# Score rows of single-head layers through VectorE and DRAM instead of TensorE, and a second, transposed load of adj

## Chip, cores, metric

The kernel runs on one core of a Trainium2 chip. The metric is device time in microseconds for one launch over all 128 graphs; the number compared is the median of repeated runs.

## What is computed

There are 128 graphs of 128 nodes with 512 features, x[128, 128, 512], and an integer adjacency matrix adj[128, 128, 128]. Each graph goes through four attention layers, every one of the form x = x + layer(relu(layernorm(x))). All is float32.

```
h = relu(layernorm(x))
layer 0:  s[i,j] = leaky(f1[i] + f2[j]), f = h W^T a;  masked where adj == 0;  softmax over j;  x += elu(att @ h)
layer 1:  4 heads of 256: s[i,j] = leaky(src[i] + dst[j]); mask adj > 0 or i == j; softmax over the SOURCE i
          (so the mask is needed transposed);  y = elu(att^T @ (h W1) + b1)
          then one head of 512 on y, same mask;  x += that + b2
layer 2:  one head: leaky(h.w_src[i] + h.w_dst[j] + b); mask adj + eye != 0; softmax over j;  x += att @ h
layer 3:  8 heads of 64: leaky(a_src[i] + a_dst[j] + b); mask adj > 0; softmax over j;  x += relu(att @ (h Wp))
```

## The kernel before

**Staging.** Weights stay in SBUF. One graph at a time is a *stream*: the generator `graph(b)` (line 920) yields single instructions (`Step`), groups of them, and takes of buffers. Up to FLYING = 11 graphs are in flight, and a twelfth is loaded ahead. All x tiles are 128 nodes (partitions) by 512 features.

**What sets the order.** No instruction is placed by hand. A greedy planner, `Scheduler` (line 140), keeps for every engine the time at which it comes free and for every tile the time at which it is written, both from cost formulas in `Step.estimate` (line 61). `issue()` (line 241) takes, out of the next steps of all streams, the one that can start first; a tie goes to the stream with the earlier due time (`rank`), and due times come from a rehearsal of one graph. What it emits is a fixed order for each engine; at run time each engine waits in that order. The transfers of SP (plain DMAs) and POOL (accumulating DMAs) are part of it: SP too executes its DMA issues in order and waits before each for its data. In the planner all transfers share one pipe (`moved`).

**Score rows.** A score needs f2[j] along the free axis, in all 128 partitions. There are two ways in the kernel:
- *TensorE*: a transpose of the column broadcast to 128 columns gives the row in a PSUM bank. `attended` (line 667) does so for layers 0, 2 and the second part of layer 1, and `add_rows` (line 587) for eight or sixteen columns at the end.
- *DRAM*: `rows_in_dram` (line 567) transposes 32x32 squares on VectorE, writes them to DRAM with four small DMAs, and a DMA broadcasts the result to 128 partitions. The four heads of layer 1 and the heads of layer 3 use this, except in the last LATE = 5 graphs.

`attention` (line 614) then adds row and mask and takes the maximum on VectorE (one operation with an accumulator for each head: a tensor_tensor_reduce, which the profile lists as CUSTOM_DVE_ANT_0 and DVE_READ_ACCUMULATOR2_ANT), and ScalarE does leaky relu and exp.

**Layer 3** (line 822) holds two times eight heads of 128x128 in one tile `sd`: `d` (rows by mask, for the maximum) and `e` (transposed). ScalarE copies the masks into both halves, one POOL DMA of 1024 KB adds all sixteen rows onto them with accumulation, VectorE reduces `d` to the maximum mx, and a second POOL DMA adds -mx onto `e`.

**Masks.** adj is loaded for four graphs at once (`load`, line 904). m0, m3 and m2 come from it on VectorE; the transposed masks m1 and m3t come from one TensorE transpose of m3 (lines 929 to 937). m3t lives from layer 1 to layer 3, in 11 buffers.

**Norm.** `norm_relu` (line 502): statistics on VectorE, reciprocal root on POOL, then nmr = -mean x rstd on VectorE, relu with scale and bias on ScalarE.

**Turn.** After layer 1's softmax `turned` (line 547) transposes the squares on VectorE and exchanges them through DRAM (four writes `turned<-e`, one read `et<-turned`).

**Buffers** that the text names: h (4), x2 (2; the projected y of layer 1's second part, held until its attention is done), e0 (3), r (5), sd (3).

Of the kernel before, what the change touches and what calls it, by code (L numbers as in the profile page):

```python
# [21 lines left out]
FLYING = 11  # L22
AHEAD = 1
# [19 lines left out]
class Step:  # L43
# [4 lines left out]
    def __init__(self, engine, method, args, kw):  # L48
        self.engine = engine
        self.calls = [(method, args, kw)]  # L50
        named = dict(kw)
        outs = [named.pop("out")] if "out" in named else [args[0]]
        if "accum_out" in named:
            outs.append(named.pop("accum_out"))
        ins = list(args[1:] if "out" not in kw else args) + list(named.values())
        ins = [a for a in ins if isinstance(a, bass.AP)]
        self.writes = [a.tensor.name for a in outs]
        self.reads = [a.tensor.name for a in ins]
        self.busy, self.delay = self.estimate(method.__name__, outs, ins, kw)

    def estimate(self, name, outs, ins, kw):

        if name == "dma_start":
            moved = size(outs[0]) * outs[0].shape[0] * 4
            if self.engine == "POOL":
                self.moves = moved / 165e3
                return 1.0, 3
            run = 4 * min(a.shape[-1] for a in outs + ins)
            self.moves = moved / (280e3 if run > 512 else 220e3)
            return (0.5 if max(len(a.shape) for a in outs + ins) > 2 else 0.35), 1.5  # L70
# [68 lines left out]

class Scheduler:  # L140
    def __init__(self):
        self.streams = []
        self.engine_free = {}
        self.written = {}
        self.moved = 0.0
        self.returned = {}
        self.tag_of = {}
        self.last_use = {}
        self.reached = set()
        self.pace = 0.0  # L150
        self.due = None
# [80 lines left out]
    def start(self, step):  # L232
        t = self.engine_free.get(step.engine, 0.0)
        for r in step.reads:
            t = max(t, self.written.get(r, 0.0))
        for w in step.writes:
            if w not in self.last_use:
                t = max(t, self.written.get(w, 0.0))
        return t

    def issue(self):
# [5 lines left out]
        if not ready:  # L247
            assert not self.streams, [vars(s.next) for s in self.streams]
            return False
        t, _, _, _, s = min(  # L250
            (self.start(s.next), self.rank(s), s.age, i, s) for i, s in enumerate(ready)
        )
        step = s.next
# [4 lines left out]
        end = t + step.busy + step.delay  # L258
        if step.moves:

            self.moved = max(end, self.moved) + step.moves
            end = self.moved + 0.3
        for name in step.writes:
            self.written[name] = end
        for name in step.reads + step.writes:
            self.last_use[name] = max(end, self.last_use.get(name, 0.0))
# [17 lines left out]
def kernel(  # L284
# [40 lines left out]
    small = ctx.enter_context(tc.tile_pool(name="small", bufs=FLYING + 2))  # L325
# [17 lines left out]
    def column(tag, n=1):  # L343
        return small.tile([P, n], F32, tag=tag, name=tag)

# [5 lines left out]
    off_diag = const.tile([P, P], F32, name="off_diag")  # L351
    nc.vector.tensor_scalar(off_diag, ident, -1.0, 1.0, ALU.mult, ALU.add)
# [36 lines left out]
    def setup():  # L389
# [6 lines left out]
        w0 = yield tile_of("sd", 3, 2 * H3, P)  # L396
        w0 = w0.rearrange("p s q -> p (s q)").rearrange("p (c f) -> p c f", c=KC)
        for c in range(KC):
            yield S.dma_start(out=w0[:, c], in_=l0_w[c * P : (c + 1) * P])
# [4 lines left out]
        yield Fork(fold_w1())  # L404
        yield from load(1)
# [19 lines left out]
        wa = yield tile_of("sd", 3, 2 * H3, P)  # L425
        wa = wa.rearrange("p s q -> p (s q)")[:, : H3 * 2 * K3]
# [5 lines left out]
    def fold_u(w0):  # L432
        us = [(yield bank()), (yield bank())]
        for c in range(KC):
            for i, u in enumerate(us):
                yield T.matmul(
                    u,
                    lhsT=a0[:, c, i : i + 1].to_broadcast([P, P]),
                    rhs=w0[:, c, :],
                    start=(c == 0),  # L440
                    stop=(c == KC - 1),
                )
# [3 lines left out]
        give_back(w0)  # L446
# [39 lines left out]
    def fold_w3(wa):  # L486
        pairs = wa.rearrange("p (h k) -> p h k", h=H3)
        for w in wpx:
            for s in range(2):
                prod = yield tile_of("t3", 2, D)  # L490
# [11 lines left out]
    def norm_relu(xt):  # L502
# [9 lines left out]
        yield V.scalar_tensor_tensor(nmr, mean, -1.0, rstd, ALU.mult, ALU.mult)  # L512
# [69 lines left out]

    def repeated(cols):
        n = cols.shape[1]
        return cols.unsqueeze(1).to_broadcast([P, Q // n, n])

    def add_rows(cols, to):

        for g in range(0, cols.shape[1], 4):
            pt = yield bank()  # L590
            yield Group(
                [
                    T.transpose(
                        pt[:, j * P : (j + 1) * P],
                        cols[:, g + j : g + j + 1].to_broadcast([P, P]),
                        ident,
                    )
                    for j in range(4)
                ]
            )  # L600
# [4 lines left out]
    def added(cols, to, late, rows=None):  # L605

        if late:
            yield from add_rows(cols, to)
            return
        if rows is None:  # L610
            rows = yield from rows_in_dram(repeated(cols), cols.shape[1])
        yield G.dma_start(out=to, in_=rows, accum_op=ALU.add)

    def attention(own, rows, e, mask, exact=False):
# [4 lines left out]
        mx = column(f"mx{nh}", nh)  # L619
# [18 lines left out]
        neg = column(f"neg{nh}", nh)  # L638
        yield V.scalar_tensor_tensor(neg, mx, -1.0, own, ALU.mult, ALU.subtract)
        nm = column(f"nm{nh}", nh)  # L640
        yield V.scalar_tensor_tensor(nm, neg, SLOPE, neg, ALU.mult, ALU.min)
        z = column(f"z{nh}", nh)
# [20 lines left out]
        rz = column(f"rz{nh}", nh)  # L663
        yield V.reciprocal(rz, z)
        return rz

    def attended(own, other, mask, values, exact=False):

        e = yield tile_of("e0", 3, P)
        pb = yield bank()  # L670
        yield T.transpose(pb[:, :P], other.to_broadcast([P, P]), ident)
        rz = yield from attention(own, [pb[:, :P]], [e], mask, exact)
# [5 lines left out]
        return pa, rz  # L678
# [39 lines left out]
    def layer0(xt, mask):  # L718
        h = yield from norm_relu(xt)
        yield Until("u")  # L720
        f = column("f0", 2)
        yield from dot(h, u1, f[:, 0:1])
        yield from dot(h, u2, f[:, 1:2])
        t = yield tile_of("t0", 2, D)
        pa, rz = yield from attended(f[:, 0:1], f[:, 1:2], mask, h, exact=True)
        give_back(h)

        yield A.activation(out=t, in_=pa, func=AF.Exp, scale=rz)
        yield A.activation(out=pa, in_=pa, func=AF.Relu, scale=rz)
        yield V.scalar_tensor_tensor(t, t, 1.0, pa, ALU.min, ALU.add)  # L730
# [4 lines left out]
    def layer1(xt, mask, late):  # L735
# [22 lines left out]
        rz = yield from attention(fx[:, H1:E1], heads, heads, mask)  # L758
        for j in range(H1):
            yield A.activation(out=heads[j], in_=heads[j], func=AF.Copy, scale=rz[:, j : j + 1])  # L760
        if late:
# [7 lines left out]
        for g in range(0, FC, 4):  # L769
# [23 lines left out]
            t = yield tile_of("t1", 2, 4 * P)  # L793
# [11 lines left out]
        pa, rz = yield from attended(gx[:, 1:2], gx[:, 0:1], mask, gx[:, E2:])  # L805
        give_back(gx)
        yield V.scalar_tensor_tensor(xt, pa, rz, xt, ALU.mult, ALU.add)
        give_back(pa)

    def layer2(xt, mask):  # L810
        h = yield from norm_relu(xt)
        f = column("f0", 2)
        yield from dot(h, w_src, f[:, 0:1])
        yield from dot(h, w_dst, f[:, 1:2])
        fb = column("fb")
        yield G.tensor_tensor(fb, f[:, 0:1], b_l2, ALU.add)
        pa, rz = yield from attended(fb, f[:, 1:2], mask, h)
        give_back(h)
        yield V.scalar_tensor_tensor(xt, pa, rz, xt, ALU.mult, ALU.add)
        give_back(pa)  # L820

    def layer3(xt, mask, mask_t, late):
# [10 lines left out]
        sd = yield tile_of("sd", 3, 2 * H3, P)  # L833
        d, e = sd[:, :H3], sd[:, H3:]
        for to, m in (d, mask), (e, mask_t):
            yield A.copy(to, m.unsqueeze(1).to_broadcast([P, H3, P]))
            give_back(m)
# [9 lines left out]
        f = small.tile([P, 2, H3], F32, tag="f3", name="f3")  # L847
        yield G.tensor_tensor(f, fx[:, :, :E3].rearrange("p h s -> p s h"), b_l3, ALU.add)
        fork = yield Fork(
            added(f.rearrange("p s h -> p (s h)"), sd.rearrange("p s q -> p (s q)"), late)  # L850
        )
        yield Join(fork)

        mx = column("mx3", H3)
        yield V.tensor_reduce(mx, d, AX.X, ALU.max)
        yield V.tensor_tensor(mx, mx, f[:, 1], ALU.add)
        yield A.activation(out=mx, in_=mx, func=AF.Prelu, alpha=SLOPE)
        yield V.tensor_scalar(mx, mx, -1.0, None, ALU.mult)
# [9 lines left out]
        rows = (yield Join(fork)) if fork else None  # L868
        fork = yield Fork(added(mx, e.rearrange("p h q -> p (h q)"), late, rows))
        yield Join(fork)  # L870
        ef = e.rearrange("p h q -> p (h q)")
        yield A.activation(out=ef, in_=ef, func=AF.Exp)
        t = yield tile_of("t3", 2, D)
        rz = column("rz3", H3)
# [24 lines left out]
        give_back(sd, fx)  # L899
# [4 lines left out]
    def load(b):  # L904
# [3 lines left out]
        if b % AG == 0:  # L908
# [3 lines left out]
            )  # L912
        sched.reached.add(("x", b))

    def not_above_0(a):
        m3 = yield tile_of("m3", 4, P)
        yield V.tensor_scalar(m3, a, 0.0, NEG, ALU.is_le, ALU.mult)
        return m3

    def graph(b):  # L920
        if FLYING + AHEAD <= b + AHEAD < B:
            yield Fork(load(b + AHEAD))
        yield Until(("x", b))
# [3 lines left out]
        yield from layer0(xt, m0)  # L927
        give_back(m0)
        m3 = yield from not_above_0(a)
        m3t = yield tile_of("m3t", FLYING, P)  # L930
        m1 = yield tile_of("m1", 8, P)
        pt = yield bank()
        yield T.transpose(pt[:, :P], m3, ident)
        give_back(m3)
        yield V.tensor_tensor(m1, pt[:, :P], off_diag, ALU.mult)
        yield A.copy(m3t, pt[:, :P])
        give_back(pt)
        yield from layer1(xt, m1, b >= B - LATE)
# [4 lines left out]
        yield from layer2(xt, m2)  # L943
        give_back(m2)
        m3 = yield from not_above_0(a)
        yield from layer3(xt, m3, m3t, b >= B - LATE)
        yield S.dma_start(out=out[b], in_=xt)

    adjs, xs = {}, {}
    with tc.manual_schedule():  # L950
        sched.rehearse(load(0))
        sched.plan(sched.rehearse(graph(0)))
# [59 lines left out]
```

## Time and profile before

| | |
|---|---|
| median of 3 runs | 3317.16 us (3317.16 to 3318.29) |
| profiled execution | 3315.37 us, of which the span of the profile is 3313.6 |
| TensorE (PE) busy | 3278.1 us, 99%; granted clock 0.992 |
| VectorE (DVE) busy | 2657.6 us, 80% |
| ScalarE (ACT) busy | 2600.8 us, 78% |
| GpSimd (POOL) busy | 954.6 us, 29% |
| DMA | 380.75 MB, 115 GB/s |
| transposes on TensorE by what they read | h 1024, e 404, f 336, x 128, m 128, mx 40 |

Busy time is the union of an engine's instructions, which overlap at their ends, so durations of a group add up to more than the engine's busy time. What an instruction occupies is read from the distance to the next start in the order of time. All lines of the page that name L256 come from the one call in the planner's `issue()`; groups are told apart by the tiles' names.

### The profile page before, as it was taken

The page shows a single profiled execution, that of the slowest core. Times are in us where ns is not written, and L with a number is a line of the kernel's source. Part 1 is how long each engine was busy: PE and PEld are TensorE (multiplying, and loading weights), DVE is VectorE, ACT ScalarE, POOL GpSimd, SP SyncE. Part 2 cuts the span into 40 slices and gives each one's busy share as a digit, 9 for nine tenths or more (in the row PEclk, how much of TensorE's full clock was granted, in tenths as well). Part 3 has the DMA queues.
Part 4 walks back from the last instruction along what each step waited for, and adds up shares of the span by engine and source line. Part 5 has one row for each costly group of instructions (what it writes and reads, how often), then busy time and mean ns, then how long its engine had stood idle before and what let it go on. Part 6 is the DMA issues. An engine that isn't in the chain of part 4 may idle for free.

```text
span 3313.6 us, 57764 instructions
## 1 busy us (share of the span) xinstructions
PE 3278.1 (99%) x16252; PEld 2577.0 (78%) x16252; DVE 2657.6 (80%) x9921; ACT 2600.8 (78%) x7060; POOL 954.6 (29%) x1791
## 2 busy tenths in 40 slices
PE   8999999999999999999999999999999999999997
PEld 5777777777777777777777777777777777777786
DVE  7778878878888888888888888788788878878866
ACT  5687887887888788788778878878887887887875
POOL 1123323332232332233233233323323323332221
PEclk8999999999999999999999999999999999999998
DMA  5155555455555545655555554555555555455441
GB/s 169 41 114 124 115 116 126 113 117 126 120 113 118 129 113 115 132 109 117 123 123 116 116 127 112 118 130 114 113 121 126 115 116 128 109 117 128 95 92 31
DMA packets 236001, 380.75 MB, mean 115 GB/s; under 512 B 57120, under 2 KB 136480, under 8 KB 219936
## 3 DMA queue, kind: packets, MB, share of 16 engines
q0 software_dynamic: 35424, 193.48, 31.2%
q1 hardware_dynamic: 196080, 183.57, 19.4%
q8 instruction: 129, 2.11, 0.3%
q14 instruction: 192, 1.57, 0.2%
q10 hardware_dynamic: 4176, 0.02, 0.1%
HBM read 309.35 MB, written 67.57 MB: 114 GB/s over the span
## 4 chain that ended last, share of the span: by engine, by line
PE 97%; DVE 2%; ACT 1%; issue 0%; POOL 0%; DMA 0%; POOLq 0%; ACTq 0%; DVEq 0%
PE bank L256 97%; DVE products L256 0%; DVE sd L256 0%; DVE t L256 0%; DVE st L256 0%; ACT sd L256 0%; DVE e L256 0%; DVE xt L256 0%; ACT ht L256 0%; POOL st L256 0%; DVE wpx L256 0%; DMA a<-in_L_gnn_a_dram 0%; DVE mx L256 0%; ACT h L256 0%; DVE m L256 0%
## 5 line engine op out<-in xcount | busy, mean ns | idle before, releaser
L256 PE MATMUL bank<-w2x,y 128*128 128x257 f32 x4096 | 971.8, 380 | 0.0
L256 PE MATMUL bank<-w1x,ht 128*128 128x344 f32 x3072 | 952.3, 453 | 0.0
L256 PEld LDWEIGHTS bank<-w2x,y 128*128 128x128 f32 x4096 | 740.2, 190 | 86.7 <-issue 2.6
L256 PEld LDWEIGHTS bank<-w1x,ht 128*128 128x128 f32 x3072 | 574.5, 191 | 245.9 <-issue 1.9
L256 POOL TENSOR_SCALAR st<-st 128x1 f32<-128x1 f32 x512 | 193.5, 378 | 1754.9 <-DVE st L256 1525.3
L256 PE MATMUL bank<-wpx,ht 128*128 128x264 f32 x2048 | 502.2, 389 | 1.4 <-ACT ht L256 1.4
L256 PEld LDWEIGHTS bank<-wpx,ht 128*128 128x128 f32 x2048 | 391.5, 192 | 119.2 <-issue 57.9
L256 ACT ACTIVATE h<-xt,st 128x512 f32<-128x512 f32 x512 | 415.8, 812 | 19.8 <-DVE st L256 18.2
L256 ACT COPY xl<-bank 128x344 f32<-128x344 f32 x384 | 170.9, 445 | 300.3 <-PE bank L256 300.2
L256 ACT ACTIVATE sd<-sd,f 128x128 f32<-128x128 f32 x1024 | 375.4, 393 | 0.0
L256 ACT ACTIVATE e<-e,nm 128x128 f32<-128x128 f32 x896 | 355.4, 399 | 6.8 <-DVE e L256 2.4
L256 DVE BATCH_NORM_STATS2 st<-xt 128x6 f32<-128x512 f32 x512 | 352.2, 688 | 0.0
L256 POOL TENSOR_TENSOR st<-st,minus_half 128x1 f32<-128x1 f32 x512 | 338.4, 661 | 42.4
L256 POOL DMA_DIRECT2D sd<-d x246 | 233.8, 951 | 192.8 <-DMA d<-r 161.0
L256 PEld LDWEIGHTS bank<-x,sd 128*128 128x128 f32 x2048 | 259.9, 193 | 17.4 <-ACT sd L256 8.1
L256 PE MATMUL bank<-et,xl 128*128 128x128 f32 x2048 | 272.1, 276 | 0.6 <-DMA et<-turned 0.6
L256 PEld LDWEIGHTS bank<-et,xl 128*128 128x128 f32 x2048 | 261.0, 193 | 11.7 <-issue 1.9
L256 PE MATMUL bank<-x,sd 128*128 128x65 f32 x2048 | 258.1, 269 | 7.1 <-ACT sd L256 7.1
L256 DVE SCALAR_TENSOR_TENSOR xt<-bank,rz,xt 128x512 f32<-128x512 f32 x256 | 191.5, 748 | 90.2 <-PE bank L256 90.1
L256 PE MATMUL bank<-h,et 128*128 128x512 f32 x512 | 245.6, 598 | 2.1 <-ACT et L256 2.1
L256 DVE STREAM_TRANSPOSE e<-e 128x512 f32<-128x512 f32 x123 | 87.5, 711 | 153.0 <-ACT e L256 152.8
L256 ACT ACTIVATE e<-e,rz 128x128 f32<-128x128 f32 x512 | 188.4, 393 | 20.9 <-DVE nm L256 18.8
(93 smaller groups left out, 5500.2 us busy)
## 6 DMA issues: line engine op xcount, KB each, us to landing
sd<-d POOLq DMA_DIRECT2D x123, 1024.0 KB, 10.3
sd<-d POOLq DMA_DIRECT2D x123, 512.0 KB, 5.1
xt<-in_x_dram SPq DMA_DIRECT2D x128, 256.0 KB
e<-d SPq DMA_DIRECT2D x128, 256.0 KB
out_dram<-xt SPq DMA_DIRECT2D x128, 256.0 KB
turned<-e SPq DMA_DIRECT2D x492, 64.0 KB
et<-turned SPq DMA_DIRECT2D x123, 256.0 KB
at<-in_adj_dram SPq DMA_DIRECT2D x32, 256.0 KB
```

The source lines that it names most:

```text
L256: method(*args, **kw)
```

## The change

- **Rows**: `attended` gets a `late` flag. In graphs that are not late the row comes from the new `row()`: a VectorE transpose of the column's 32-wide broadcast, one small DMA to DRAM, one broadcast DMA of 64 KB into a tile `row` (3 buffers), from which VectorE reads. Late graphs keep TensorE's transpose.
- **adj**: `load_turned` loads adj of four graphs a second time, with the 32x32 squares exchanged (four DMAs whose runs are 32 integers), and VectorE transposes all squares in place, once for four graphs. m1 and m3t come from this tile. TensorE's transpose of m3 and ScalarE's copy to m3t are gone.
- **Layer 3**: the `d` half is no longer pre-filled with the mask and accumulated; SP broadcasts the eight rows into a tile `d3` (2 buffers) and VectorE adds the mask and takes the maximum, one operation for each head. Only the `e` half (`e3`, 3 buffers) is accumulated by POOL. The addition to mx and its negation go to POOL.
- **Norm**: nmr moves from VectorE to POOL.
- **Small tiles**: the column tiles of a pool come from explicit buffers (`c`, `f0`, `f3`), and t0, t1, t3 share one tag `t` of 5.
- **Planner**: `issue()` first picks the engine whose step can start first, then on VectorE and ScalarE takes the most urgent step that can start within PATIENCE = 0.3 us of it. Transfers are kept in a list by the time at which they reach the queue, and SP and POOL may have LANES = 8 in flight each. Costs of transfers are changed.

```diff
 def start(self, step):
     t = self.engine_free.get(step.engine, 0.0)
+    if step.moves:
+        t = max(t, self.lanes[step.engine][len(step.calls) - 1].end)
...
-        t, _, _, _, s = min(
-            (self.start(s.next), self.rank(s), s.age, i, s) for i, s in enumerate(ready)
+        _, _, i = min((self.start(s.next), self.rank(s), i) for i, s in enumerate(ready))
+        engine, soon = ready[i].next.engine, self.start(ready[i].next)
+        if engine in ("DVE", "ACT"):
+            soon += PATIENCE
+        _, _, i = min(
+            (self.rank(s), s.age, i)
+            for i, s in enumerate(ready)
+            if s.next.engine == engine and self.start(s.next) <= soon
         )
...
-        yield V.scalar_tensor_tensor(nmr, mean, -1.0, rstd, ALU.mult, ALU.mult)
+        yield G.tensor_scalar(nmr, mean, rstd, -1.0, ALU.mult, ALU.mult)
...
+    def row(col):
+        r = yield tile_of("r", 5, Q)
+        yield V.transpose(r, col.to_broadcast([P, Q]))
+        d = dram.tile([R, Q], F32, tag="d1", name="d")
+        yield S.dma_start(out=d, in_=r[::Q])
+        give_back(r)
+        to = yield tile_of("row", 3, P)
+        yield S.dma_start(out=to, in_=d.rearrange("c b -> (c b)").partition_broadcast(P))
+        return to
...
-    def attended(own, other, mask, values, exact=False):
+    def attended(own, other, mask, values, late, exact=False):
         e = yield tile_of("e0", 3, P)
-        pb = yield bank()
-        yield T.transpose(pb[:, :P], other.to_broadcast([P, P]), ident)
-        rz = yield from attention(own, [pb[:, :P]], [e], mask, exact)
+        if late:
+            rows = yield bank()
+            yield T.transpose(rows[:, :P], other.to_broadcast([P, P]), ident)
+        else:
+            rows = yield from row(other)
+        c, rz = yield from attention(own, [rows[:, :P]], [e], mask, exact)
...
-        sd = yield tile_of("sd", 3, 2 * H3, P)
-        d, e = sd[:, :H3], sd[:, H3:]
-        for to, m in (d, mask), (e, mask_t):
-            yield A.copy(to, m.unsqueeze(1).to_broadcast([P, H3, P]))
-            give_back(m)
+        e = yield tile_of("e3", 3, H3, P)
+        yield A.copy(e, mask_t.unsqueeze(1).to_broadcast([P, H3, P]))
+        give_back(mask_t)
...
+        if late:
+            fork = yield Fork(add_rows(f[:, 1], e.rearrange("p h q -> p (h q)")))
+        else:
+            rows = yield from rows_in_dram(repeated(f.rearrange("p s h -> p (s h)")), 2 * H3)
+            d = yield tile_of("d3", 2, H3, P)
+            yield S.dma_start(out=d.rearrange("p h q -> p (h q)"), in_=rows[:, : H3 * P])
+            fork = yield Fork(added(e.rearrange("p h q -> p (h q)"), rows[:, H3 * P :]))
+        for g in range(0, H3, 4):
+            if late:
+                d = yield from spread(f[:, 0, g : g + 4])
+                part = d.rearrange("p (h q) -> p h q", h=4)
+            else:
+                part = d[:, g : g + 4]
+            yield Group(
+                [
+                    V.tensor_tensor_reduce(
+                        out=part[:, j], in0=part[:, j], in1=mask, scale=1.0, scalar=LOWEST,
+                        op0=ALU.add, op1=ALU.max, accum_out=mx[:, g + j : g + j + 1],
+                    )
+                    for j in range(4)
+                ]
+            )
...
-        mx = column("mx3", H3)
-        yield V.tensor_reduce(mx, d, AX.X, ALU.max)
-        yield V.tensor_tensor(mx, mx, f[:, 1], ALU.add)
+        yield G.tensor_tensor(mx, mx, f[:, 1], ALU.add)
         yield A.activation(out=mx, in_=mx, func=AF.Prelu, alpha=SLOPE)
-        yield V.tensor_scalar(mx, mx, -1.0, None, ALU.mult)
+        yield G.tensor_scalar(mx, mx, -1.0, None, ALU.mult)
...
+    def load_turned(b):
+        adjs_t[b // AG] = t = adjp.tile([P, AG, P], I32, tag="at_t", name="at_t")
+        yield Group(
+            [
+                S.dma_start(
+                    out=t[m * Q : (m + 1) * Q].rearrange("b g (r c) -> b (g r) c", r=R),
+                    in_=adj[b : b + AG, :, m * Q : (m + 1) * Q].rearrange(
+                        "g (r b) c -> b (g r) c", r=R
+                    ),
+                )
+                for m in range(R)
+            ]
+        )
...
-        m3 = yield from not_above_0(a)
-        m3t = yield tile_of("m3t", FLYING, P)
-        m1 = yield tile_of("m1", 8, P)
-        pt = yield bank()
-        yield T.transpose(pt[:, :P], m3, ident)
-        give_back(m3)
-        yield V.tensor_tensor(m1, pt[:, :P], off_diag, ALU.mult)
-        yield A.copy(m3t, pt[:, :P])
-        give_back(pt)
+        at = adjs_t[b // AG]
+        if b % AG == 0:
+            flat = at.rearrange("p g j -> p (g j)")
+            yield V.transpose(flat, flat)
+            sched.reached.add(("adj_t", b // AG))
+        yield Until(("adj_t", b // AG))
+        at = at[:, b % AG, :]
+        m1 = yield tile_of("m1", 9, P)
+        yield V.scalar_tensor_tensor(m1, at, 0.0, neg_off_diag, ALU.is_le, ALU.mult)
```

## The prediction

> **What bounds the kernel now.** I read the busy shares first, then the chain of waits, then the table by stretches. In the last one the columns are: the stretch, its length, and the busy time of PE, PE's weight loads, VectorE (DVE), ScalarE (ACT) and GpSimd (POOL), then PE's clock, the DMA share and GB/s.
>
> ```profile
> PE 3278.1 (99%) x16252; PEld 2577.0 (78%) x16252; DVE 2657.6 (80%) x9921; ACT 2600.8 (78%) x7060; POOL 954.6 (29%) x1791
> ...
> 82.75 3128.28 PE bank L256 x15535
> ...
> 0.00:83.00 83.00, 66.92 (x246) 44.15 (x247) 59.92 (x225) 45.47 (x121) 13.41 (x35) 0.82 0.56 169
> ...
> 1100.00:1600.00 500.00, 500.00 (x2487) 393.50 (x2486) 407.94 (x1531) 401.85 (x1096) 150.91 (x279) 1.00 0.54 119
> ...
> 3211.00:3313.60 102.60, 83.20 (x473) 69.80 (x471) 69.18 (x196) 55.69 (x137) 15.60 (x37) 0.90 0.19 47
> ```
>
> The second line says that from 82.75 us, for 3128.28 us, the chain never leaves PE. The fourth shows 500 us of 500. Only the ramp (16.1 us of PE idle) and the drain (19.4 us) hold anything else. A busy PE could still be slow within itself, so I price what is removed by spacing in the order of time, not by duration:
>
> ```profile
> 1502.78 0.28 PE L256 MATMUL bank<-ident,e 128*128 128x128 f32 x1
> 1502.89 2.48 PE L256 MATMUL bank<-w1x,ht 128*128 128x344 f32 x8
> ...
> 1518.67 0.27 PE L256 MATMUL bank<-ident,m 128*128 128x128 f32 x1
> 1518.79 0.27 PE L256 MATMUL bank<-ident,x 128*128 128x128 f32 x1
> 1518.89 1.90 PE L256 MATMUL bank<-w2x,y 128*128 128x257 f32 x8
> ```
>
> A single transpose lasts 0.27 us but the next instruction starts 0.10 to 0.12 us after it: it costs PE 0.11 us. The same w2x group recurs at 1500.20 and 1525.33, so one graph takes 25.13 us. Scaled to that period, VectorE is busy 20.5 us, ScalarE 20.2, GpSimd 7.6.
>
> **What the Trainium skill says.** "Perfetto Trace Analysis", section Optimizing Scalar/DVE Operations: profiled latency is about twice what an operation occupies its engine, since the write acknowledgement overlaps the next instruction. The trace agrees for small ones (0.16 us long, 0.07 apart) and less for a reduction over 128x128 (0.29 long, 0.21 apart, below). "DMA: Bandwidth & Descriptors", section Anatomy of one DMA: about 2 us fixed per DMA on GpSimd's path, mostly the receipt of the write. On SP's path the trace has a VectorE transpose ending at 1518.73 and, after four small writes, the GpSimd transfer that reads them at 1522.01: 3.3 us with 1.3 us of issuing in it, so about 2 us here too. Same page, Specifications: line rate wants pieces of at least 512 B; the new load of adj has 128 B pieces, and no run here shows its rate.
>
> **The change, part by part.**
>
> *PE.* Before, 336 transposes read f, 128 read x (names of the program with numbers left out; 123 of these 128 belong to graphs that are not late), 128 read m. In the 123 graphs not late, layers 0 and 2 drop one each (246), layer 1 drops one (123); all 128 graphs drop the mask transpose. 246+123+128 = 497, times 0.11 us = **54.7 us** off PE (0.10 and 0.12 give 49.7 and 59.6). Period 25.13 - 4x0.11 = 24.69 us. In the late graphs spread() does the transposes that add_rows() did for the d half: no change of count.
>
> *VectorE.* These rows carry the spacing:
>
> ```profile
> 1508.93 1.22 DVE L256 TENSOR_REDUCE mx<-sd 128x8 f32<-128x1024 f32 x1
> 1510.06 0.28 DVE L256 CUSTOM_DVE_ANT_0 e<-e,m 128x128 f32<-128x128 f32 x1
> 1510.27 0.08 DVE L256 DVE_READ_ACCUMULATOR2_ANT mx<- 128x1 f32 x1
> 1510.27 0.29 DVE L256 CUSTOM_DVE_ANT_0 e<-e,m 128x128 f32<-128x128 f32 x1
> ...
> 1511.85 0.21 DVE L256 STREAM_TRANSPOSE r<-mx 128x32 f32<-128x32 f32 x1
> 1511.98 0.12 DVE L256 SCALAR_TENSOR_TENSOR neg<-mx,xl 128x4 f32<-128x4 f32 x1
> ```
>
> Per graph: eight mask-and-maximum operations instead of one wide reduction, 8x0.21 - 1.13 = +0.55; three row transposes 3x0.13 = +0.39; a quarter of the 128x512 transpose of adj, 0.63/4 = +0.16; four nmr to GpSimd, -4x0.07 = -0.28; the add and the negation of mx to GpSimd, -0.15. The first mask becomes m3t's mask (0.13 each); m1 costs 0.20 from a bank and 0.20 from SBUF. Sum +0.67: 21.2 us of 24.69, **86%**. With full durations instead it is +1.56, 22.1 us, 89%. Both stay under PE.
>
> *ScalarE.* Loses one 128x1024 copy (0.93 to 1.05) and the m3t copy (0.16): about -1.1, to 19.1 us, 77%. *GpSimd.* Gains four 128x1 operations at 0.38, an add bounded by the 0.61 of 128x16, a negation of about 0.4: +2.5, to 10.1 us, 41%. The norm's chain loses the hop to VectorE and back, on which VectorE waited 32.6 us in all. The two accumulating transfers stay in number (0.95 us of issue each); the first now moves half.
>
> *SP and DMA.* In one period SP waits 15.4 us and issues for 9.7. Added: six row transfers at 0.3 to 0.35, the d load 0.34, and one of four adj_t transfers per graph, from 0.57 (the load of adj) to 2.1 (the longest write of turned): +2.9 to +4.4, so 51 to 57% of a period. Bytes:
>
> ```profile
> q0 software_dynamic: 35424, 193.48, 31.2%
> q1 hardware_dynamic: 196080, 183.57, 19.4%
> ```
>
> 64.5 MB (123 x 512 KB) go from q0 at 0.161% per MB to q1 at 0.106%: -3.6 points. Rows: 24.2 MB, +2.6 (4.7 by packets). adj_t is 65,536 packets: +0.9 by bytes, +6.5 by q1's mean per packet. The DMA share goes from 54% to between 54 and 62%. One adj_t load is, by the same two prices, 0.3 to 8 us of the queue every four graphs.
>
> *The new wait.* Before, a score row was a 0.11 us transpose; now it is a transpose on VectorE, a write of 512 B and a broadcast of 64 KB, with SP waiting in order for each: my estimate is 5 us, the 3.3 us above less three write issues (about 1 us) and some 2.5 us for the broadcast (512 KB land in 5.1 us, and this is an eighth of it), up to 8 with SP held by something else (its longest wait for an r is 14.7). Behind a waiting SP queue stand the rows of other graphs and turned/et; behind a late row on VectorE stands everything on VectorE, then PE. What hides it: eleven graphs in flight, 276 us each, of which 3x5 us is 5%. Where cover is thinnest is **x2, two buffers**. I read from the order of time: a graph's first w2x group starts one period before the one at 1518.89, so at about 1493.8; its second part is added at 1514.95; its transpose is at 1518.79, its x,et product at 1505.21+25.13 = 1530.34, end 1531.3. It holds x2 for some 37.5 us of two periods, 50.3 before and 49.4 after; plus 5 to 8 is 42.5 to 45.5. It fits with 4 to 7 us to spare. The transposed e also waits for PE, so some of the 11 us after the transpose can shrink.
>
> *Order.* PATIENCE lets VectorE and ScalarE wait up to 0.3 us for an older graph's step, and the transfers are modelled one by one. PE is saturated already, so I cost this at 0; it could take away bubbles of ramp and drain (a few us) or make new ones (up to 0.3 us a step, 11% of VectorE's time is left for them).
>
> *Ends.* The ramp gets the row waits while weight loads fill the queue, and one adj_t load: bounds -5 to +10, I take +5. The drain keeps PE transposes; VectorE saves 1.36 - 0.55 per late graph: 0. Bubbles in the steady part, mostly rows behind an adj_t load: 31 loads at 0 to 1 us, I take 5.
>
> *Sum.* 3313.6 - 54.7 + 5 + 5 = 3268.9 of span. The profiled execution took 3315.37, 1.8 over its span, and the median shown is 3317.16, 1.8 over that: 3268.9 + 3.6 = 3272.5, given as **3272 us**.
>
> **The rivals.** *x2 holds PE (slower).* If a row costs layer 1 more than 12 us (behind an adj_t load of up to 8 us and an SP that waits), x2 passes two periods and the period becomes half the hold. Break-even with before is 50.26-37.5 = 12.8 us; at 15 us the period is 26.25, 123x1.12 = +138, 3455 us; at 13.5 some 3360. For it: two in-order DMA hops, 128 B pieces. Against it: SP's mean wait is far below its longest, and the slack after the transpose. *VectorE gives it back.* At 86 to 89% in a fixed order a late VectorE shows up in PE as bubbles; 0.3 us a graph would be 37 us: 3308 us. For it: VectorE already sits 152.8 us waiting for ScalarE's e, time that a fixed order can't fill, so its free share is smaller than it looks. Against: at 80% VectorE makes PE wait for nothing in 3128 us. *Row traffic is hidden and the ramp improves:* no additions, 3255 us or a little lower. *That the edit does not act:* excluded, the 497 instructions are not issued.
>
> **How the numbers follow.** PE stays the bound with small losses: 0.70, range 3250 to 3298. VectorE or transfers give most back: 0.10, 3298 to 3324, half of it over 0.2% better than before. x2 or late rows: 0.20, 3324 to 3455. 0.2% is 6.6 us, about what a measurement of this kernel can tell from no change. Faster 0.75, same 0.05, slower 0.20. Range 3250 to 3330: 3 in 100 below, about 17 above.
>
> **What would show it.** Right: ident,f 90 times, ident,x 5, no ident,m; PE busy near 3223 us; steady stretches still 500 of 500 and 24.7 us between equal w2x groups; VectorE near 430 of 500. Wrong: PE waiting in the steady part for VectorE's e or x; VectorE waiting for the DMA of row; a period above 25.1; the DMA share above 65%.

## The result, and the profile after

The changed kernel takes **3460.21 us** (median of 4 runs, 3455.03 to 3461.19) against 3317.34 before: ratio 1.0427, 95% interval 1.041 to 1.0443. The forecast was 3272.

The busy shares, and the top of SP's own list of waits (who waited for whom, us in total, times, longest; in the third fence the line of before):

```profile
PE 3290.7 (95%) x15755; PEld 2536.5 (73%) x15755; DVE 2742.2 (79%) x11464; ACT 2442.2 (71%) x6804; POOL 1071.5 (31%) x2559
```

```profile
SPq L301 <- DMA d<-r: 688.5, 471, 6.0
SPq L301 <- DVE r L301: 529.7, 242, 12.0
```

```profile
SPq L256 <- DMA d<-r: 115.4, 168, 2.1
```

The removal happened: 16252 - 15755 = 497 instructions fewer on PE. But PE's busy time went up by 12.6 us, where the sum took 54.7 off, and its idle time from 35.5 us (3313.6 - 3278.1) to 168.7 (3459.4 - 3290.7). Together that is the span's 145.8 us. At the top of SP's list is now the wait for its own small writes. VectorE has a wait that before's list does not hold at all, for the broadcasts of rows: `row` is that of a single-head layer, `d<-d` that of the eight rows of layer 3 (512 KB), which is new too:

```profile
DVE e L301 <- DMA row<-d: 148.1, 121, 3.6
DVE d L301 <- DMA d<-d: 133.7, 85, 4.6
```

Two numbers locate it. The issues of the 128 results on SP give the time of the first result (the ramp) and, between 500 and 3050 us, the time for one graph. First the line of before, then that of after (count, durations in ns, first and last start):

```profile
L256 SPq DMA_DIRECT2D out_dram<-xt x101: 350/357/359, 524.6 to 3037.5; - x101
```

```profile
L301 SPq DMA_DIRECT2D out_dram<-xt x98: 350/360/1484, 511.3 to 3037.3; - x98
```

Before: 2512.9/100 = 25.13 us a graph; after: 2526.0/97 = **26.04**, where 24.69 was worked out. The first result comes at 225.1 instead of 201.3: **23.8 us** lost in the ramp. Stretches of after (columns as in the prediction):

```profile
0.00:83.00 83.00, 50.63 (x174) 32.93 (x175) 49.12 (x155) 25.08 (x57) 9.22 (x33) 0.69 0.60 164
1100.00:1600.00 500.00, 484.21 (x2330) 373.74 (x2329) 405.13 (x1704) 364.58 (x1016) 161.39 (x383) 1.00 0.54 126
```

In the steady part PE is idle for 16 us of 500, where before there was nothing. One such pause, of 2.16 us, in the order of time: VectorE first stands for a broadcast, and PE then stands for a statistic of VectorE's. After it comes the granted clock around the pause (the third column from the end):

```profile
1497.10 0.29 DVE L301 CUSTOM_DVE_ANT_0 d<-d,m 128x128 f32<-128x128 f32 x1 [3.58 <-DMA d<-d]
...
1502.70 0.33 PE L301 MATMUL bank<-ident,e 128*128 128x128 f32 x1 [2.16 <-DVE st L301]
1502.87 0.60 PE L301 MATMUL bank<-ident,h 128*128 128x128 f32 x4
1503.30 3.17 PE L301 MATMUL bank<-wpx,ht 128*128 128x264 f32 x8
1506.27 1.53 PE L301 MATMUL bank<-h,et 128*128 128x512 f32 x2
...
1526.59 1.94 PE L301 MATMUL bank<-wpx,ht 128*128 128x264 f32 x8
1528.37 1.05 PE L301 MATMUL bank<-et,xl 128*128 128x128 f32 x8
```

```profile
1498.00:1502.00 4.00, 2.54 (x14) 1.81 (x12) 3.84 (x22) 1.07 (x4) 1.52 (x3) 1.00 0.00 0
1502.00:1508.00 6.00, 5.30 (x17) 3.77 (x18) 5.53 (x27) 5.08 (x16) 1.74 (x4) 0.72 0.48 144
1508.00:1514.00 6.00, 6.00 (x27) 4.59 (x26) 4.28 (x20) 5.18 (x20) 3.22 (x8) 1.00 0.49 91
```

Eight wpx instructions take 2.97 us to the next start after the pause and 1.78 us later on: over 6 us the granted clock is 0.72 in the mean. This pause cost more than its own length. Others did not: after a longer one, of 2.97 us, the clock stayed at 1.00.

```profile
2024.57 0.33 PE L301 MATMUL bank<-ident,e 128*128 128x128 f32 x1 [2.97 <-DVE st L301]
```

```profile
2024.60:2032.00 7.40, 7.01 (x29) 4.99 (x30) 6.96 (x33) 6.63 (x22) 3.15 (x6) 1.00 0.30 91
```

Between 500 and 3050 us the clock falls only five times, to half for 3.4 us each. Over the whole span the mean granted clock, 0.984 against 0.992, makes some 29 us (3459.4 x 0.016 - 3313.6 x 0.008), less than half of the 67 us by which PE is busy for longer than worked out (12.6 + 54.7). Another part, as an estimate, is the end of the instruction before each pause, which no next one covers: 0.16 us (0.27 - 0.11) at some 140 more pauses than before, 22 us. The rest stays open.

### The profile page after: what moved, and what is told of

The parts are those of the page before. It is cut to its first block, busy times and chain, and to the rows that moved or that the text cites. A ratio compares the mean times of both kernels' runs of the same rounds, so it can differ in the third digit from the quotient of the medians.

```text
span 3459.4 us, 60112 instructions
## 1 busy us (share of the span) xinstructions
PE 3290.7 (95%) x15755; PEld 2536.5 (73%) x15755; DVE 2742.2 (79%) x11464; ACT 2442.2 (71%) x6804; POOL 1071.5 (31%) x2559
## 3 DMA queue, kind: packets, MB, share of 16 engines
q14 instruction: 217, 1.78, 0.2%
## 5 line engine op out<-in xcount | busy, mean ns | idle before, releaser
L301 ACT ACTIVATE e<-e,c 128x128 f32<-128x128 f32 x1408 | 537.7, 398 | 116.1 <-DVE c L301 98.3
L301 POOL TENSOR_SCALAR st<-st 128x1 f32<-128x1 f32 x1024 | 297.5, 297 | 1021.7 <-DVE st L301 425.6
L301 ACT ACTIVATE e<-e,f 128x128 f32<-128x128 f32 x1152 | 416.0, 392 | 64.2 <-DVE c L301 61.0
L301 POOL DMA_DIRECT2D e<-d x246 | 232.3, 946 | 376.8 <-DMA d<-r 260.8
L301 DVE CUSTOM_DVE_ANT_0 d<-d,m 128x128 f32<-128x128 f32 x984 | 232.0, 290 | 134.4 <-DMA d<-d 133.7
L301 PEld LDWEIGHTS bank<-x,e 128*128 128x128 f32 x2048 | 265.2, 193 | 60.4 <-issue 34.8
L301 DVE CUSTOM_DVE_ANT_0 products<-h,u 128x512 f32<-128x512 f32 x256 | 176.5, 690 | 142.7 <-ACT h L301 138.9
L301 PE MATMUL bank<-x,e 128*128 128x65 f32 x2048 | 262.7, 272 | 16.3 <-ACT e L301 6.5
L301 POOL TENSOR_SCALAR m<-m 128x128 f32<-128x128 f32 x128 | 82.4, 644 | 483.3 <-DVE c L301 266.4
L301 DVE CUSTOM_DVE_ANT_0 e<-row,m 128x128 f32<-128x128 f32 x369 | 102.2, 277 | 148.9 <-DMA row<-d 148.1
```

Of the source, the lines that this page charges most:

```text
L301: method(*args, **kw)
```

## The experiments

The body is the part of the program that says what is computed, the planner the part that orders it. Theory R: the two DMA hops of each row hold up SP, then VectorE, then PE. Theory P: the planner's new rules make a worse order, whatever the body. Theory G: nmr stands behind GpSimd's waits. Every ratio is to before.

**1. The planner alone, the body alone, nmr, rows.**

```diff
 e1: before.py, with Step ... Scheduler of after, PATIENCE and LANES
 e2: after.py, with Step ... Scheduler of before
 e3: after.py
-        yield G.tensor_scalar(nmr, mean, rstd, -1.0, ALU.mult, ALU.mult)
+        yield V.scalar_tensor_tensor(nmr, mean, -1.0, rstd, ALU.mult, ALU.mult)
 e4: after.py, in attended
-        if late:
+        if True:
```

> The kernel of before with the planner of after (PATIENCE, LANES, the list of transfers, the costs of transfers), nothing else. Theory R (the two DMA hops of each score row hold up SP and then VectorE): the planner costs nothing by itself, within 10 us of before, 3307 to 3327. Theory P (the new rule of order opens bubbles): this is slower than before by much of the 143 us, 3380 to 3460. Theory G (nmr on GpSimd stands behind GpSimd's other waits): like R.

> The body of after with the planner of before, costs of transfers included. R: about as slow as after or slower, since the old planner knows still less of transfers in flight: 3440 to 3600. P: near the 3272 predicted, 3260 to 3320. G: about as after, 3440 to 3480.

> After, with nmr computed on VectorE again. G: ScalarE's 159 us of waiting in h for GpSimd's st and VectorE's 141 us in products go, a gain of 50 to 120 us, 3340 to 3410. R: GpSimd's waits were not what ended last, within 25 us of after, 3435 to 3475. P: the same.

> After, with the score rows of the single-head layers by TensorE's transposes in all graphs as in before (and the transpose of adj planned only once its load is); all else of after stays: 369 transposes of 0.11 us, 41 us, come back on TensorE. R: TensorE saturated again: 3317 less 14 us of mask transposes, 3295 to 3330. G: nmr is still on GpSimd, 3400 to 3470. P: the order rule is still there, 3420 to 3500.

Measured: e1 **3427.27** (1.0329; 1.0314 to 1.0344), e2 3399.13 (1.0247), e3 3396.89 (1.0233), e4 3350.71 (1.0097). Each of four edits seems to hold a large part of the 143 us, and they add up to far more. The surest reading is e1: **the planner alone, on the old body, costs 109 us.** Time per graph there is 26.00 us with PE's work unchanged. So R alone is not enough, and P is half right: something in the planner is bad. In e1 SP waits no longer for its small writes than in before (117.6 us against 115.4). VectorE does the standing, for the broadcasts of layer 1's rows (`e<-d`), a wait that before's list does not hold:

```profile
SPq L301 <- DMA d<-r: 117.6, 160, 2.0
```

```profile
DVE e L301 <- DMA e<-d: 233.4, 104, 3.7
```

e2 says the old planner does not make the new body fast either: it meets none of the three theories' ranges, and VectorE waits there 298 us for broadcasts of rows (254.9 for `row<-d`, 43.3 for `d<-d`). e4 is above R's range and below those of G and P.

**2. Which rule of the planner?** The transfers' costs hold one number that can be read against the trace: a small write on SP is planned to be issued in 0.35, to land 0.6 later, with 0.3 on top: 1.25 us, or more when the planner's list has larger transfers ahead of it. In after, SP's `d<-r` is in 46 places between 600 and 3000 us a single write directly followed by `row<-d`, which waits for a write like it. From the one issue to the other these places fall into two groups with nothing in between: 23 take 1.88 to 2.42 us, and 23 take 5.08 to 6.67 us. In each of the longer ones, and in none of the shorter, the 512 KB broadcast `d<-d` was issued 2.0 to 2.4 us before the write. If the broadcast of the row waits for the write just ahead of it, this is the write's landing; if for an earlier one, that one took longer still. A place of each group:

```profile
1541.38 0.33 SPq L301 DMA_DIRECT2D d<-d  x1
1543.07 0.32 SPq L301 DMA_DIRECT2D row<-d  x1
1543.44 1.07 SPq L301 DMA_DIRECT2D d<-r  x1
1548.52 0.31 SPq L301 DMA_DIRECT2D row<-d  x1
...
1558.31 0.50 SPq L301 DMA_DIRECT2D d<-r  x1
...
1560.48 0.34 SPq L301 DMA_DIRECT2D row<-d  x1
```

```diff
 e5: after.py        e9: e1
-            return busy, (2.2 if moved > 16384 else 0.6)
+            return busy, (2.2 if moved > 16384 else 1.6)
 e6: e1              e7: after.py
-PATIENCE = .3
+PATIENCE = 0.0
```

> After, with one number of the planner changed: a small write on SP is taken to land 1.6 us after its issue instead of 0.6. Theory W (SP stands 689 us before the broadcast reads because the planner orders them for a write that lands too early): SP's wait for d<-r falls below 300 us and the period from 26.0 to 25.4 or less, 3360 to 3400. Theory L (the two hops are too long whatever the order; buffers or the static order of VectorE decide): within 25 us of after, 3435 to 3480.

> The kernel of before with the planner of after, but PATIENCE 0 instead of 0.3, so an engine again takes the step that can start first. If the patience makes the 109 us that this planner cost the body of before: 3310 to 3340. If the new model of the transfers makes them: 3400 to 3440.

> After, with PATIENCE 0. If patience costs after what it may cost before (about 100 us, nearly one for one): 3340 to 3380. If the two hops of the rows decide and patience matters only where PE was saturated: 3420 to 3470.

> The kernel of before with the planner of after, in which a small write is taken to land 1.6 us after its issue instead of 0.6 (before's own planner had 1.5 for every transfer on SP). If that number makes the 109 us that the planner cost this body: 3305 to 3335. If the list of transfers, the lanes or the other costs make them: 3390 to 3430.

e5: **3348.29** (1.0097; 1.0079 to 1.0114), a gain of 112 us by one number that no instruction carries: only the order changed. It is more than expected, while SP's wait for d<-r, at 426.0 us, stays above the 300 expected. e9: 3336.69 (1.0053): the planner's cost on the old body falls from 109 us to 19, and VectorE's wait from 233.4 us to 17.5:

```profile
DVE e L301 <- DMA e<-d: 17.5, 11, 5.1
```

PATIENCE is not the cause: without it both are slower, e6 3449.04 and e7 3477.72. The lanes, the list and the other costs were not run apart; on the old body they and PATIENCE together are left with the 19 us.

**3. A dose, or a lucky order?**

```diff
 e13: after.py, 1.1 instead of 0.6        e14: after.py, 2.6 instead of 0.6
```

> After, a small write taken to land 1.1 us after its issue. If the planner's number acts as a dose (each exchange planned too short costs what it is short by): between 3348 (1.6) and 3460 (0.6), 3380 to 3430. If any change of the number shuffles the order and 1.6 was a lucky one: anywhere, and not between.

> After, a small write taken to land 2.6 us after its issue, later than the trace shows. Dose: a plan that expects too much loses little, within 25 us of the run with 1.6, 3325 to 3375. Luck: far from it, over 3390.

| planned landing of a small write | us | us a graph | SP's wait for d<-r | VectorE's wait for row<-d and d<-d |
|---|---|---|---|---|
| 0.6 (after) | 3460.21 | 26.04 | 688.5 | 281.8 |
| 1.1 (e13) | 3387.65 | 25.49 | 447.4 | 163.8 |
| 1.6 (e5) | 3348.29 | 25.25 | 426.0 | 99.7 |
| 2.6 (e14) | 3324.15 | 24.86 | 144.1 | 11.9 |

Each later landing is faster than the one before it, and both waits fall along: a dose, over these four points. Of the two waits only VectorE's also tells e1 from before. The steady part of e14:

```profile
L301 SPq DMA_DIRECT2D out_dram<-xt x103: 337/356/357, 502.2 to 3038.1; - x103
...
600.00:3100.00 2500.00, 2499.01 (x12185) 1956.12 (x12184) 2123.16 (x8995) 1926.57 (x5348) 892.12 (x2019) 1.00 0.55 131
```

PE is saturated again, and a graph takes 2535.9/102 = 24.86 us, with the rows through DRAM as in after: of the 0.44 us predicted per graph, 0.27 are there. The same exchanges that made PE wait in after are hidden once a write is planned at 2.6 + 0.65 = 3.25 us, between the two lengths measured.

**4. The ramp.** In after, SP sends the first writes of rows behind all weights, and the broadcasts behind twelve transfers of adj_t:

```profile
35.07 1.77 SPq L301 DMA_DIRECT2D xt<-in_x_dram  x3
36.98 1.84 SPq L301 DMA_DIRECT2D d<-r  x3
38.95 7.31 SPq L301 DMA_DIRECT2D at_t<-in_adj_dram  x12
46.30 1.44 SPq L301 DMA_DIRECT2D row<-d  x3
```

```profile
56.11 0.47 PE L301 MATMUL bank<-ident,e 128*128 128x128 f32 x1 [16.29 <-ACT e L301]
```

```profile
53.72 0.69 DVE L301 TENSOR_REDUCE wpx<-t 128x8 f32<-128x512 f32 x1
54.33 0.28 DVE L301 CUSTOM_DVE_ANT_0 e<-row,m 128x128 f32<-128x128 f32 x1
```

PE stands 16.29 us until the first row has gone through VectorE and ScalarE. When the row itself landed does not show: VectorE takes it at 54.33 without a pause, straight after its share of preparing the weights (wpx), which stands ahead of it in the order.

```diff
 e8: after.py
-        yield Fork(load_turned(0))
+        yield from load_turned(0)         # and so for the later ones
 e10: e8 with 1.6, and attended's flag
+        pe = late or (b < 6 and sched.due is not None)
 e16: after.py with 1.6; b < 12: rows and masks by TensorE, no load_turned
```

> After, with the transposed load of adj issued in its place among the other loads (yield from instead of Fork), so SP sends it at about 8 us and not at 38 us behind all weights. If the late issue makes the 24 us by which the first result is later (225 against 201): 3430 to 3445, first result at 200 to 208. If the row exchanges in the ramp make them: 3455 to 3465.

> After with 1.6 for a small write, and a mended ramp: the transposed adj is loaded in its place, and the first 6 graphs take their score rows by TensorE. If rows and adj queued on SP behind the weights make the late first result (231 in the run with 1.6 alone): first result at 195 to 210 and 3315 to 3330. If only the weights' own arrival sets it: within 8 us of 3348.

> After with 1.6, and the first 12 graphs take rows and transposed masks by TensorE as before, with no transposed load ahead of them. If rows and the load of adj make the whole ramp loss: first result at 199 to 205, and 3348 less some 25, 3310 to 3330. If something else in the new body makes it: first result still over 210.

e8 3451.15: the first result stays at 225.5, so adj_t's place alone is not it. In e4, with rows by TensorE, it was 220.9: nor is it the rows alone. e5, with 1.6 and nothing else, has 230.8; e10 brings it to 214.1, e16 to **203.3**: rows and adj_t together make the late first result. But the totals, 3353.02 and 3344.94, gain nothing or little over e5's 3348.29, against the 18 to 38 us expected: what the ramp gives is given back in the rest.

**5. Rows and nmr again, planned with 1.6.**

```diff
 e11: e10, rows by TensorE in all graphs        e12: e10, nmr on VectorE
```

> The same with all graphs' single score rows by TensorE: 0.33 us more a graph on TensorE, two hops fewer three times a graph. If the two hops still cost PE more than 0.33 us a graph once they are planned rightly: period 25.0 to 25.1, 3295 to 3312, faster than the run with rows through DRAM. If they are hidden: period 0.2 to 0.3 longer than there, 3320 to 3350.

> The mended ramp and 1.6, rows through DRAM, nmr on VectorE again. If GpSimd's order (nmr behind its waits) costs by itself: 20 to 60 us faster than with nmr on GpSimd, 3265 to 3305. If the 63 us that the same edit brought to after were a chance of the order there: within 15 us of that run.

e11 3336.24, 17 us faster than e10: in this pair, with 1.6, the hops still cost more than the transposes they save. e12 3375.05, 22 us *slower* than e10, while the same edit gained 63 us in e3, within G's range: G does not hold under the second plan. The sign of that edit depends on the plan around it.

**6. A part that gains, and the mended kernel.** In e4, e10, e11, e12 and e15 to e18 VectorE's transpose of adj is planned after its load, by one line that after lacks; their figures include it.

```diff
 e15: before.py and its planner; b >= 12: m1, m3t from load_turned; t0, t1, t3 as t (5), m3t 3 buffers
 e17: e16 with 2.6 instead of 1.6
 e18: e17
-            return busy, (2.2 if moved > 16384 else 2.6)
+            return busy, (3.2 if moved > 16384 else 2.6)
```

> The kernel of before, its planner too, with one part of the change alone: from the thirteenth graph on, the transposed masks come from the second load of adj and VectorE's squares (t0, t1 and t3 share 5 buffers, m3t has 3, to make room). TensorE loses 116 transposes of 0.11 us, 13 us. If the 128 B pieces of that load don't matter: 3300 to 3312. If they hold up SP or the queue: 3320 to 3350.

> After with 2.6 us for a small write (3324) and the ramp as in before (first result at 203 instead of 229). If the two losses are separate, they add: 3324 less 26, 3290 to 3305, faster than before and after. If the gain in the ramp is given back in the steady part or the drain, as with 1.6: 3315 to 3325.

> The same with 3.2 instead of 2.2 us for larger transfers on SP too. If the broadcast of a row is planned too short as the write was: a period nearer 24.7 and 5 to 20 us less than the run before. If 2.2 was long enough: within 8 us of it.

e15 3320.97 (1.0011; 1.0002 to 1.002): a graph takes 25.07 us instead of 25.13, where one transpose less (0.11) was dropped, and yet the whole is no faster; the first twelve graphs transpose m3 twice there, so PE has 104 instructions fewer, not 116. e17 **3320.7** (1.0008; 1.0000 to 1.0016): level with before, so the gains in the ramp and in the steady part do not add up; no run was faster than before. A graph takes (3030.8 - 520.9)/101 = 24.85 us, but the first result is at 211.6 and PE is idle for 60.9 us in all (3316.9 - 3256.0) against 35.5 before. e18 **3455.11**: one more microsecond for the larger transfers costs 134 us, 26.15 us a graph, where at most 20 us of gain or 8 of change were expected. VectorE waits only 22 us for broadcasts of rows there and SP 143.2 us for d<-r, so neither wait makes it. Planning too long is no safe side; why this one hurts so much stays open, with this one plan.

## Why the prediction was wrong, point by point

- **PE's saving: the size right, the time not there.** 497 instructions left. In e14 and e17 0.27 to 0.28 of the 0.44 us a graph are seen in a saturated steady part. ident,x stands 5 times and ident,m not at all; ident,f stands 130 times, as the 40 transposes of mx now read the tile f too (90 + 40).
- **The load of VectorE and ScalarE and the DMA share: right.** In after VectorE's 405.13 of 500 us at 26.04 us a graph is 21.1 us (21.2 predicted), ScalarE 19.0 (19.1), the DMA share 0.54 (0.54 to 0.62). GpSimd was overrated: 8.4, not 10.1. None of them is full. VectorE does give the gain back, though not by being too busy, as the rival had it, but by standing in its fixed order for broadcasts.
- **The step that failed is "Order", costed at 0.** It priced PATIENCE and took the list of transfers to be a better model. The prediction had the number that speaks against it: it read about 2 us for a small write from the trace, and never held that against the planner's 0.35 + 0.6 + 0.3. The order was made for 1.25 us (or more behind larger transfers), where 1.9 to 2.4 or 5.1 to 6.7 pass; before's planner had 1.5 for every transfer of SP where after has 0.6 for small ones. VectorE is then sent to rows that have not arrived: 281.8 us in after, 233.4 in e1, none in before. The planner cost 109 us on a body whose work was unchanged, and this one number took 90 of them back (e9), and 112 to 136 us on the new body (e5, e14).
- **That is not all that an order decides.** e2 plans a small write at 0.35 + 1.5 + 0.3 = 2.15 us, near e5's 2.25, and takes 51 us more than e5; e18 keeps 2.6 and loses 134 us. In both the number for larger transfers differs as well (1.5 and 3.2 instead of 2.2), and in e2 the rest of the planner too.
- **The new wait was named, with the right path, but undersized.** "Behind a late row on VectorE stands everything on VectorE, then PE" is what happened, and two of the signs of being wrong came true: VectorE waiting for the DMA of row (148.1 us) and a period above 25.1. It was estimated at 5 us for both hops; in half of the 46 places the first alone takes that or more. The cover by eleven graphs is real (e14), but only for an order that knows the length. And layer 3's new broadcast was priced only for its issue, 0.34 us, while VectorE waits 133.7 us for it; no run puts layer 3 alone back.
- **The rival that came true in its total did not in its mechanism.** 3455 us had been worked out for x2's two buffers. In e14 the same two buffers and the same rows let PE run 2499 of 2500 us, so x2 is not what held it. That the total agrees is chance.
- **The ramp: +5 within -5 to +10; it was +23.8.** I had only looked at the queue filling up, not at the order, in which rows and adj_t come after weights on SP.
- **Slips that decide nothing.** By its own two prices one adj_t load is 0.9 to 6.7 us of the queue (0.9% and 6.5% of 3313.6 us over 32 loads), not 0.3 to 8; SP's added issues sum to 2.7 to 4.5 us, not 2.9 to 4.4. The factor of two that it took from the Trainium skill's "Perfetto Trace Analysis" (Optimizing Scalar/DVE Operations) is there that of an operation's access overhead, not of its whole length: the trace agrees, as length less spacing is nearly the same for both kinds of operation (0.16 - 0.07 = 0.09 and 0.29 - 0.21 = 0.08 us).
- **Left open:** why 2.6 leaves 0.17 us a graph above the 24.69; why 3.2 for larger transfers costs 134 us; whether rows by TensorE with 2.6 would be faster still (not run). How far a single figure can be the order's chance can be seen in nmr: -63 and +22 us for one edit.

## What to carry to other kernels

Where a planner writes a fixed order, its latencies are part of the kernel: read every one of them against the trace before pricing what the instructions do. Put a new exchange into such a plan with its measured length, from issue to the next issue that depends on it, under load, and look at the spread before taking a median: here it had two lengths. Then try more than one value, since one that was longer still lost 134 us elsewhere. Ask the trace which engine stands for the exchange in its fixed order: here it was VectorE, though SP's list was longer. And keep one edit from being judged by one order: repeat it under a second plan before calling it a gain or a loss.

## What the runs showed that I had not expected

A write of 512 B to DRAM had two lengths, by what was issued before it. Directly followed by a broadcast that waits, it stood 1.9 to 2.4 us from issue to issue in 23 places, and 5.1 to 6.7 us in the 23 places with a 512 KB broadcast ahead of it. The Trainium skill's "DMA: Bandwidth & Descriptors" (Anatomy of one DMA) gives a fixed part of about 2 us on GpSimd's path; the first group, on SP's path, is near it, the second is not, and there the runs decide. Which of the transfers ahead makes the difference was not separated. The plan with 2.6 + 0.65 was the best of four.

PE's granted clock averaged 0.72 over the 6 us from the end of a pause of 2.16 us, eight 128x264 products taking 2.97 instead of 1.78 us; after a pause of 2.97 us it stayed at 1.00. The length of a pause alone did not decide.
